# Layer 3 of a four-layer kernel: VectorE's state sums read B·dtx from PSUM, and C's spread gets one pair of banks instead of two

## The chip, the cores and the metric

The kernel runs on one core of a Trainium2 chip. Five engines work side by side, each through its own list of instructions in order: TensorE (PE, matrix products into PSUM), VectorE (DVE), ScalarE (ACT), GpSimd (POOL) and SyncE (SP), which here issues the transfers. PSUM has eight banks of 128 x 512 float32. The metric is the device time of one execution in microseconds (us), the median of several.

## The reference

Four layers follow each other on an image x of 2 x 128 channels x 64 x 64: a scan over the image in four directions, two attention layers, and a small scan over channels. The change lies in the last. There, the 128 channels of each pixel are read as 8 tokens of 16 numbers, and a selective scan runs over the 8 tokens:

```python
dA  = exp(dt[..., None] * A)
dBx = dt[..., None] * Bm[:, :, None, :] * xs[..., None]
def step(h, inp):
    dA_t, dBx_t, C_t = inp
    h = dA_t * h + dBx_t
    return h, einsum('nds,ns->nd', h, C_t)
y = ys + xs * D;  y = y * silu(z);  out = y @ out_proj_w.T
```

Each pixel has 32 inner channels with 16 states each, 512 state values per pixel and token. Behind the scan stand a group norm, a SiLU and the sum with x.

## The kernel before

Layer 3 takes the pixels in 16 chunks of 512 (8 for each image). A chunk's 8 tokens are worked in 4 steps, k = 0 to 3, of two tokens each, o = 0 and 1. A token's 512 state values times 512 pixels stand as a tile of 128 partitions x 4 groups x 512; most instructions take half of that, 128 x 1024, called half 0 or 1.

The tiles:

- D[k, o], in SBUF, is loaded from DRAM with B spread over the partitions (L1395). A product with rx turns it into B·dtx (`db_`, L1417), and a sum with A turns it into the state h (`add`, L1439). There are six buffers of it.
- rx, in PSUM, holds dt·xs of one token, spread by TensorE (`rx_`, L1413). It has two banks.
- A[k, o] is exp(dt·A) by ScalarE (`da_`, L1424). GpSimd multiplies it by the state of the token before (`mul`, L1434): A·h. This is then what the sum takes, and what is multiplied by C.
- q, in PSUM, holds C of two groups, spread by TensorE (`pc_`, L1451) for one product by C. It has two buffers of a pair of banks each.
- The product by C (`hc_`, L1457) is made in place in A, on VectorE. TensorE then sums it over the states into y (`y_`, L1467), a bank of its own. The part of y that comes from B·dtx is added apart, as (sum of C·B)·dtx (`cbx_`, `ecb_`, L1403), so that the last token's B·dtx is never needed.
- misc, one bank, takes every other matmul of the layer.

So q has four banks, rx two, y and misc one each: all eight.

The order is written out by hand. For each step s the loop goes through four groups g, and `PLAN[k][g]` names the state work in order: `m10` is GpSimd's product for token o = 1, half 0; `v10` the sum on VectorE and `g11` the sum on GpSimd, for token and half; `C` the next product by C, which belongs to the step before (`pc_` = step s-1); `D` the next product with rx, which belongs to the step after (`nc_` = step s+1). A group with a C in it first issues one more fill of q (`prepare`), ahead of the y matmuls and of what `first` lists; what `extra` lists comes behind. Each engine gets its instructions in the order in which the loop comes past them, and waits by semaphores for the others.

In a chunk there are 14 GpSimd products, 12 sums (8 on VectorE, 4 on GpSimd), 14 products with rx and 14 by C. In step k = 0 only token 1 has a predecessor within the chunk, and a product by C takes two groups of that token, whose two matmuls into q read the same 32 partitions; otherwise the two matmuls read different ones.

Transfers go by SP's queue: per step, the spread of dt (`spread`, L1383) and the loads of D for the step after the next (`load`, L1395).

## Time and profile before

| what | before |
|---|---|
| median of 3 runs | 6422.57 us (6415.79 to 6423.95) |
| the profiled execution | 6431.21 us, its span 6429.4 us |
| granted TensorE clock, whole span | 0.904 |
| busy, whole span: PE, DVE, ACT, POOL | 89%, 88%, 69%, 84% |
| layer 3, 5465.1 to 6429.4 | 964.3 us |
| busy in layer 3: PE, DVE, ACT, POOL | 834.1, 878.2, 460.9, 791.8 us |
| granted clock in layer 3 | 0.86 |

A row of a view by windows gives a stretch (us from the span's start), its length, the busy time of PE, of its weight loads, of DVE, ACT and POOL with the number of instructions, then the granted clock, the busy share of the 16 transfer engines and GB/s. A row of the groups gives line, engine, operation, tiles (written <- read), shapes and count, then the busy time in us and the mean in ns, then the idle time of the engine ahead of these instructions and what ended it. A row of the timeline gives start, duration, engine, line, tiles and shapes, and in brackets the idle time before it with what ended that. PE shows a float32 matmul of 512 columns as two records.

### The profile page before, as it was taken

The numbers are of one execution on the slowest core, as the hardware profiler recorded it, in microseconds if no ns is written. First come the engines' busy times: TensorE is split into PE (matmuls) and PEld (weight loads), VectorE is DVE, ScalarE is ACT, GpSimd is POOL, SyncE is SP. The second block draws the span as 40 slices with busy tenths as digits, with TensorE's granted clock in tenths as the row PEclk, the third lists the DMA queues.
The fourth block names the chain that finished last, engine by engine and source line by source line (L and its number), as shares of the span: only waits on it lengthen the run. The fifth ranks groups of instructions, "written<-read, shape, count | busy, mean of one in ns | idle before, by whom it ended". The sixth has DMA issues, their size and how long they took to land. (4 is left out here: it accounts for less than half of the span.)

```text
span 6429.4 us, 66778 instructions
## 1 busy us (share of the span) xinstructions
PE 5699.0 (89%) x20010; PEld 2783.6 (43%) x20010; DVE 5639.6 (88%) x4502; ACT 4413.5 (69%) x7768; POOL 5391.6 (84%) x2519
## 2 busy tenths in 40 slices
PE   8888888888888888888878999999999999888898
PEld 2222222222222222222225888888888788222221
DVE  7999999999999999999997777777777777899997
ACT  7887778877788877787776566555556665545453
POOL 6999999999999999999996677666766566888886
PEclk8888888888888988888878999999999999799887
DMA  6566666566666666666651000000000000977775
GB/s 182 144 154 168 166 152 149 147 151 151 145 149 150 156 151 152 148 155 157 153 144 42 1 5 3 1 1 1 1 1 1 2 6 7 219 184 176 182 176 123
DMA packets 400478, 700.37 MB, mean 109 GB/s; under 512 B 74089, under 2 KB 76658, under 8 KB 399730
## 3 DMA queue, kind: packets, MB, share of 16 engines
q1 hardware_dynamic: 399232, 694.33, 44.5%
q8 instruction: 157, 2.57, 0.2%
q14 instruction: 207, 1.70, 0.1%
q10 hardware_dynamic: 882, 1.78, 0.1%
HBM read 584.53 MB, written 111.28 MB: 108 GB/s over the span
## 5 line engine op out<-in xcount | busy, mean ns | idle before, releaser
L405 POOL TENSOR_TENSOR dbu<-dus,bs 128x1024 f32<-128x1024 f32 x1024 | 2463.4, 2441 | 116.6 <-DVE h L449 97.2
L449 DVE TENSOR_TENSOR_SCAN h<-da,hst,dbu 128x1024 f32<-128x1024 f32 x896 | 2088.9, 2343 | 109.5 <-ACT hst L454 46.6
L418 ACT ACTIVATE da<-dts,aneg 128x512 f32<-128x512 f32 (+1 forms) x2048 | 1411.5, 689 | 210.3 <-DVE h L449 171.2
L1028 POOL TENSOR_TENSOR sum<-sum,sc 128x1024 f32<-128x1024 f32 x378 | 898.1, 2376 | 397.9 <-ACT sc L1023 392.7
L990 ACT COPY sc<-s 128x512 f32<-128x512 f32 x1024 | 596.9, 585 | 703.2 <-PE s L985 574.9
L985 PE MATMUL s<-q,k 128*128 128x256 f32 x4096 | 1051.9, 380 | 10.3 <-ACT lo L943 5.5
L1040 PE MATMUL av<-sc,v 128*128 128x256 f32 x4096 | 1050.3, 379 | 9.1 <-ACT sc L1023 9.1
L472 PE MATMUL y<-hc,cst 128*32 128x512 f32 x4096 | 744.9, 663 | 274.3 <-DVE hc L461 245.3
L997 DVE TENSOR_TENSOR mx<-mx,s 128x512 f32<-128x512 f32 x896 | 609.8, 681 | 369.8 <-ACT sc L990 362.3
L461 DVE TENSOR_TENSOR hc<-h,pc 128x1024 f32<-128x1024 f32 x728 | 870.9, 1196 | 0.6 <-PE pc L438 0.5
L985 PEld LDWEIGHTS s<-q,k 128*128 128x128 f32 x4096 | 770.9, 190 | 124.5 <-issue 8.3
L1040 PEld LDWEIGHTS av<-sc,v 128*128 128x128 f32 x4096 | 772.1, 190 | 116.2 <-ACT sc L1023 14.4
L459 POOL TENSOR_TENSOR hc<-h,cs 128x1024 f32<-128x1024 f32 x296 | 705.1, 2382 | 1.1 <-issue 1.1
L1434 POOL TENSOR_TENSOR A<-A,D 128x1024 f32<-128x1024 f32 x224 | 526.7, 2370 | 134.3 <-DVE D L1439 100.5
L438 PE MATMUL pc<-xd,sel 16*128 16x512 f32 x1024 | 627.3, 699 | 1.3 <-DVE hc L461 1.3
L1020 DVE TENSOR_TENSOR sc<-sc,pm 128x1024 f32<-128x1024 f32 x512 | 620.7, 1213 | 2.2 <-PE pm L1015 1.7
L1023 ACT ACTIVATE sc<-sc 128x1024 f32<-128x1024 f32 x512 | 543.3, 1061 | 43.6 <-DVE sc L1020 43.4
L472 PEld LDWEIGHTS y<-hc,cst 128*32 128x32 f32 x4096 | 109.5, 112 | 805.6 <-DVE hc L461 418.4
L433 ACT ACTIVATE dbu<-hst,dbu,df 128x1 f32<-128x1 f32 x896 | 338.5, 378 | 100.3 <-POOL dbu L405 77.5
L1451 PE MATMUL q<-xs,room 32*128 32x512 f32 x840 | 287.5, 696 | 64.7 <-DVE A L1457 63.5
L438 PEld LDWEIGHTS pc<-xd,sel 16*128 16x128 f32 x1024 | 164.7, 198 | 377.4 <-issue 332.4
L449 DVE TENSOR_TENSOR_SCAN h<-da,dbu 128x1024 f32<-128x1024 f32 x128 | 290.8, 2281 | 16.0 <-POOL dbu L405 5.9
(317 smaller groups left out, 7841.9 us busy)
## 6 DMA issues: line engine op xcount, KB each, us to landing
dts<-ddt SPq DMA_DIRECT2D x512, 256.0 KB, 5.5
dus<-ddu SPq DMA_DIRECT2D x512, 256.0 KB, 5.1
D<-rows SPq DMA_DIRECT2D x448, 256.0 KB, 6.0
bs<-rows SPq DMA_DIRECT2D x1024, 64.0 KB, 4.9
cs<-rows SPq DMA_DIRECT2D x1024, 64.0 KB, 3.3
ddt<-dt SPq DMA_DIRECT2D x128, 256.0 KB, 2.0
ddu<-dtu SPq DMA_DIRECT2D x128, 256.0 KB, 4.1
dtr<-ddt SPq DMA_DIRECT2D x448, 64.0 KB, 2.1
```

What stands on the lines that cost most here:

```text
L405: nc.gpsimd.tensor_mul(t, self.dus[q], _bc(self.bs[g], 1, [P, 2, T]))
L418: act(t[:, i, sl], self.dts[q][:, i, sl], AF.Exp, scale=an[:, g, 2 * q + i : 2 * q + i + 1])
L438: mm(t, lhsT=sel[32:48, 4 * g : 4 * g + 4, :].rearrange("p n d -> p (n d)"), rhs=self.xd[32:48, :], start=True, stop=True)
L449: nc.vector.tensor_tensor_scan(ho, ai, bi, init, ALU.mult, ALU.add)
L459: nc.gpsimd.tensor_mul(t, self.h[u], _bc(self.cs[gq(u)[0]], 1, [P, 2, T]))
L461: nc.vector.tensor_mul(t, self.h[u], _bc(self.pc[u // 2], 1, [P, 2, T]))
L472: mm(self.y[q // 2][r : r + 32, :], lhsT=sum4, rhs=self.hc[u][:, i, :], start=False, stop=(u % 8 >= 6), skip_group_check=True)
L985: mm(p[:, o, :], lhsT=j.k[m // 8][:, m % 8 * P : m % 8 * P + P], rhs=self.q, start=True, stop=True)
L997: nc.vector.tensor_max(self.mx, self.s[0][:, 0:2, :] if u == 1 else self.mx, self.p[u])
L1020: nc.vector.tensor_sub(s, s, _bc(self.pm[:, :], 1, [P, 4, NQ]))
L1028: self.adds.tensor_add(self.sum, self.s[0] if w == 1 else self.sum, self.s[w])
L1040: mm(self.av, lhsT=self.job.v[m // 8][:, m % 8, :], rhs=self.s[u // 2][:, m % 4, :], start=(m == 0), stop=(m == 31))
```

## The change

VectorE's sum no longer finds B·dtx in D. The product with rx is made directly ahead of it, in the token's own step, and writes a new PSUM tile dd of two banks; the sum reads dd and A and writes D. For tokens and halves whose sum is GpSimd's, and for a chunk's first token, the product still works in place in D: it is named `d` when it belongs to the own step, `n` when it is the first token of the next chunk. The banks for dd come from q, which has one pair now. A fill of q is issued directly behind the product by C that empties the pair, instead of ahead of the group. rx is filled one token at a time, token 1 at the own step's group 0, token 0 at group 2 of the step before. `PLAN` has 9 sums on VectorE and 3 on GpSimd, in a new order.

```diff
-            def db_(self, k, o, half):
-                d = self.D[k, o][:, 2 * half : 2 * half + 2, :]
-                nc.vector.tensor_mul(d, d, _bc(self.rx[k, o], 1, [P, 2, T]))
+            def db_(self, k, o, half, own=False):
+                d = t = self.D[k, o][:, 2 * half : 2 * half + 2, :]
+                if own:
+                    t = self.dd = ps.tile([P, 2, T], F32, tag="dd", name="dd")
+                nc.vector.tensor_mul(t, d, _bc(self.rx[k, o], 1, [P, 2, T]))
...
-                eng.tensor_add(d, d, self.A[k, o][:, g, :])
+                eng.tensor_add(d, self.dd if eng is nc.vector else d, self.A[k, o][:, g, :])
...
-                q = self.q[k, u] = ps.tile([P, 2, T], F32, tag="q", name="q", bufs=2)
+                q = self.q[k, u] = ps.tile([P, 2, T], F32, tag="q", name="q")
...
         PLAN = (
-            ("m10 m11 C D", "C D time", "C v10 D", "g11 D C"),
-            ("m00 m01 C D v00", "C v01 D m10 m11", "v10 D", "g11 D"),
-            ("m00 m01 C D v00", "C v01 m10 m11", "C v10 D", "g11 C"),
-            ("m00 m01 C D", "C v00 D g01 m10 m11", "C D", "D C"),
+            ("m10 m11 C", "v10 C time", "v11 C", "C"),
+            ("m00 m01 C v00", "v01 m10 m11 C", "v10", "d11 g11"),
+            ("m00 m01 C v00", "C v01 m10 m11", "C v10", "C d11 g11"),
+            ("m00 m01 C v00", "d01 g01 m10 m11 C", "n0 C", "n1 C"),
         )
...
+                if k == 3 and nc_ is not None:
+                    more((3, 0), lambda: nc_.rx_(0, 0), at=first)
+                elif k < 3:
+                    if cc is not None:
+                        more((k, 0), lambda: cc.rx_(k, 1), at=first)
+                    if nc_ is not None:
+                        more((k, 2), lambda: nc_.rx_(nk, 0), at=first)
...
-                    more((k, 3), lambda: n2.rx_(n2k, 0), lambda: n2.rx_(n2k, 1))
...
-                    if "C" in ops:
-                        prepare()
...
                             c_.hc_(k_, u_)
                             used += 1
-                        elif o == "D":
-                            nc_.db_(nk, nd // 2, nd % 2)
-                            nd += 1
+                            prepare()
+                        elif o[0] == "n":
+                            nc_.db_(0, 0, int(o[1]))
+                        elif o[0] == "d":
+                            cc.db_(ck, int(o[1]), int(o[2]))
...
                         else:
+                            if o[0] == "v":
+                                cc.db_(ck, int(o[1]), int(o[2]), own=True)
                             cc.add(ck, int(o[1]), int(o[2]), V if o[0] == "v" else G)
```

More of the change, by code (lines that the diff above doesn't have):

```diff
@@ L1575, in conv_seq_kernel @@
                 c.load(0, o)
-            for o in range(2):
-                c.rx_(0, o)
             c1.xs = xs1
@@ L1639, in conv_seq_kernel @@
                         more(at_, lambda j=j: nrm.store(j, (G, V)[j % 2]))
-                nd = 0
                 for g in range(4):
@@ L1646, in conv_seq_kernel @@
                     if nc_ is None:
-                        ops = [o for o in ops if o != "D"]
+                        ops = [o for o in ops if o[0] != "n"]
                     if cc is None:
-                        ops = [o for o in ops if o[0] not in "mvg"]
-                    if "C" in ops:
-                        prepare()
+                        ops = [o for o in ops if o[0] not in "mvgd"]
                     if pc_ is not None and pk and g:
```

## The prediction

> **What bounds the kernel now.** I read first the busy shares and the strip of 40 slices: layer 3 is the last 964 us (5465 to 6429), VectorE (DVE) is its fullest engine, and the granted clock (PEclk) is uneven there.

> ```profile
> DVE  7999999999999999999997777777777777899997
> POOL 6999999999999999999996677666766566888886
> PEclk8888888888888988888878999999999999799887
> ```

> Then one chunk by windows, from one VectorE product L1403 to the same product of the next chunk; behind it, two stretches with the clock in them.

> ```profile
> 5803.86:5859.61 55.75, 50.60 (x160) 12.61 (x158) 54.07 (x42) 28.66 (x34) 49.48 (x21) 0.91 0.85 190
> 5808.40:5811.80 3.40, 1.65 (x6) 0.30 (x4) 3.40 (x5) 2.75 (x4) 3.29 (x2) 1.00 0.71 164
> 5811.80:5815.20 3.40, 3.40 (x8) 0.69 (x6) 3.40 (x4) 1.80 (x2) 3.40 (x2) 0.50 1.02 230
> 5839.10:5842.50 3.40, 1.29 (x4) 0.46 (x6) 3.40 (x4) 2.28 (x3) 3.40 (x2) 1.00 1.08 213
> 5842.50:5849.40 6.90, 6.90 (x14) 1.43 (x12) 6.85 (x4) 3.86 (x4) 5.52 (x3) 0.51 0.60 131
> ```

> A chunk takes 55.75 us, of which VectorE works 54.07, TensorE 50.60, GpSimd (POOL) 49.48: VectorE sets the pace and the two others are close. A 3.4 us stretch in which TensorE is busy half or less (1.65, 1.29) is followed by one or two at a clock of 0.5.

> Third, the groups of lines in layer 3, shapes kept apart.

> ```profile
> L1434 POOL TENSOR_TENSOR A<-A,D 128x1024 f32<-128x1024 f32 x224 | 526.7, 2370 | 134.3 <-DVE D L1439 100.5 <-DMA dtr<-ddt 28.7 <-DMA D<-rows 3.8
> L1439 DVE TENSOR_TENSOR D<-D,A 128x1024 f32<-128x1024 f32 x128 | 297.9, 2327 | 5.2 <-POOL A L1434 4.6
> L1457 DVE TENSOR_TENSOR A<-A,q 128x1024 f32<-128x1024 f32 x224 | 268.6, 1209 | 14.5 <-PE q L1451 14.5
> L1417 DVE TENSOR_TENSOR D<-D,rx 128x1024 f32<-128x1024 f32 x224 | 268.4, 1210 | 31.6 <-PE q L1451 15.7 <-DMA D<-rows 13.9 <-PE rx L1413 2.0
> L1439 POOL TENSOR_TENSOR D<-D,A 128x1024 f32<-128x1024 f32 x64 | 184.3, 2879 | 3.7
> ```

> The sum on VectorE (L1439, both operands in SBUF) takes 2327 ns; the products of the same size with one operand in PSUM take 1210. Last, single rows of the timeline.

> ```profile
> 5804.99 2.36 POOL L1439 TENSOR_TENSOR D<-D,A 128x1024 f32<-128x1024 f32 x1
> 5805.60 2.83 DVE L1439 TENSOR_TENSOR D<-D,A 128x1024 f32<-128x1024 f32 x1
> ...
> 5803.08 0.67 DVE L1472 TENSOR_TENSOR sz<-sz,y 128x512 f32<-128x512 f32 x1
> 5803.86 0.70 DVE L1403 TENSOR_TENSOR y<-e,misc 128x512 f32<-128x512 f32 x1
> ...
> 5816.64 1.22 DVE L1417 TENSOR_TENSOR D<-D,rx 128x1024 f32<-128x1024 f32 x1 [1.42 <-PE q L1451]
> ...
> 5823.63 1.98 PE L1451 MATMUL q<-xs,room 32*128 32x512 f32 x4
> ...
> 5842.26 1.85 PE L1451 MATMUL q<-xs,room 32*128 32x512 f32 x4 [2.11 <-DVE A L1457]
> ...
> 5849.52 1.13 PE L1451 MATMUL q<-xs,room 32*128 32x512 f32 x4
> 5850.57 1.06 PE L1467 MATMUL y<-A,cst 128*32 128x512 f32 x6
> 5851.56 1.13 PE L1451 MATMUL q<-xs,room 32*128 32x512 f32 x4
> ```

> GpSimd's sum ends at 5807.35 and VectorE's, begun in the meantime, at 5808.43, 1.08 later: it stood until GpSimd was through. L1403 overwrites what L1472 read, and starts 0.11 after its end, where products without such a tie start 0.08 before the end of the last: a tie on VectorE costs 0.19. A TensorE item (a pair for q, the rows of one y) takes a slot of 1.03 at full clock ((5851.56-5849.52)/2), twice that at half; a q pair for a chunk's first token, whose two matmuls share rows, 1.91.

> **The change, part by part.** (a) VectorE's sums read dd in PSUM. Eight a chunk go from 2.33 to 1.13 (1.21 less the overlap of 0.08): -9.6. A ninth comes from GpSimd: +1.13 here, -2.88 there; the other three there fall from 2.88 to about 2.35. Each of the nine sums waits for its own product, a tie: 9 x 0.19 = +1.7. VectorE's work in a chunk: 14 products by C and 14 by dtx at 1.13, 9 sums at 1.13, 1.7 of ties, and 4.2 of smaller ones (yg, ecb twice, cb, bn): 47.5. GpSimd's 19 operations come to 19 x 2.36 = 45. The price of a write to PSUM in this shape is not in the trace; nearest is L1403, which writes y there at 696 ns against 678 of L1472, so between 0 and 0.04 a product; I take 0.

> [...]

> (b) One pair of banks for q. The refill can start only when the product by C (I number them C1 to C14 from step k=1 on) is through. From the rows: refill starts 0.06 after the end of C, the next C 0.03 after the recorded 1.13 of the refill: C_next = refill start + 1.16 (2.01 for a first token). But the refill also stands behind what TensorE is given between two refills. VectorE's cover is what it has to do between two Cs: 2.45 for a product and its sum, 1.13 for a product in place. I walk one chunk, clock full, taking the later of (previous C + 1.13 + cover) and the refill, whose start is the later of (previous C + 1.27) and (previous refill + its slot + 1.03 per item between):
> - C2, C3: cover 6.3 and 3.6, no wait (C2 at 7.43, C3 at 12.14).
> - C4: six items ahead of its refill (xs, y0, two sz, two rx), and 0.8 in which one of them waits for ScalarE to empty misc (the timeline has 0.78 for it at 5835.00): refill at 8.70 + 7 x 1.03 + 0.8 = 16.71, ready 17.87. GpSimd is later: the product d11 ends at 12.2, only then GpSimd's g11 and m00 (2 x 2.35) run, so add v00 starts at 16.95 where VectorE was ready at 14.55. Wait 2.40, C4 at 18.12.
> - C5: y and two xr ahead: 0.29. C6, C7: none (C7 at 28.43).
> - C8: the same chain d11, g11, m00, less 0.65 for bn: 1.75.
> - C9, C10: cover 1.13 (n0, n1), one and two items: 0.17 and 0.83. C11: cover none, y and y0 ahead: 1.96.
> - C12: y, rx, bc ahead of a cover of 2.45: 0.54. C13: none. C14: cover 0.6: 0.70.
> - next C1: no cover, a first token's refill: 2.15.

> Waits for TensorE 6.64, for GpSimd 4.15, with 47.5 of work: 58.3 a chunk, +2.55. TensorE's slots (31 items and 14 refills, 48) and GpSimd's 45 both fit into it; it is the hand-over between the three that is long. Behind a waiting C stand VectorE's product and sum, for which GpSimd's next product waits; behind a waiting refill stand y and the small matmuls that ScalarE reads, which is half idle (28.66 of 55.75) and covers that.

> (c) rx goes out one at a time, seven a chunk, where three pairs and a single shared rows' time before; it is in the item counts above. Moving products a step later gives the D loads 10 us more (13.9 us of waits in the layer, under 1 a chunk, at most that is won; I take 0, the loads being issued where they were). SP's queue and ScalarE's get nothing new.

> (d) The clock. The walk leaves TensorE idle 2.8 us before the refill after C2, and 4.5 before the one after C8. By the windows above (half idle in 3.4 us) the second falls to 0.5 for certain, the first in some 8 of 10 positions of the stretch. One stretch of 3.4 us at half loses 1.7: after C8 that lands on C10 and C11, which have no cover (+1.7); after C2 on the six items before C4, of which GpSimd's wait hides 0.25 (0.8 x 1.45 = 1.2). I take +2.9 a chunk; bounds 0 and, with two stretches each as after 5842.5, 6.6. The 55.75 of before holds its own such stretches.

> [...]

> Sum: 58.3 + 2.9 - 55.75 = +5.45 a chunk, times 15 (of 16, the last has no successor to prepare) = +82. The profiled execution took 6431.2 (span 6429.4): 6513. It stands 8.6 above the median 6422.6, so 6504 there.

> **The rivals.**
> - Faster. VectorE's freed time is kept: the three chains through GpSimd and TensorE overlap better than my walk. It decides where waits fall below 55.75 - 47.5 = 8.25 a chunk. With no wait for GpSimd and four rx beside other matmuls (as 5815.48 shows rx beside q), the walk gives 54.2 without half clock: -1.55 x 15 = -23, 6400. For it: the lock on the sums is plain. Against: C11 and C1 have no cover, 4.1 by themselves, and half clock stretches occur already before.
> - No change: full clock throughout and no wait for GpSimd gives 55.8, within 0.2% (the least that a measurement here tells from nothing; 6410 to 6435).
> - Slower still: TensorE at half clock for two stretches each time: 58.3 + 6.6 - 55.75 = 9.15 x 15 = +137, 6560. For it: 5842.5 to 5849.4. Against: 5811.8 lasted one.
> - The sums do not get shorter: were dd read as slowly as D (2.33), 9 x 1.12 more work, 10.1, less the waits that it covers (at most 10.8): between +82 and +233, 6504 to 6655. Against: L1457 and L1417 at 1.21 beside a busy GpSimd.

> **How the numbers follow.** Forecast and its neighbours (6435 to 6540) 0.65; half clock worse, 0.14; sums not shorter, 0.02; no change 0.06; faster 0.13. That gives slower 0.81, same 0.06, faster 0.13. Range 6432 to 6565: it leaves out the faster case and most of no change, and takes in the bounds of the clock.

> **What would show it.** Right: VectorE's sums at about 1.21 and GpSimd's at 2.36; products by C idle behind q for 100 us or more in the layer, against 14.5; VectorE's sums waiting 40 to 80 for GpSimd, against 5; chunks at 60 to 62; VectorE's share of layer 3 lower, a granted clock at or under 0.86 there. Wrong: chunks under 55, or q refilled before VectorE asks for it at C11 and C1; then the walk's coupling is not there.

## The result

The changed kernel takes 6567.57 us (median of 4 runs, 6559.99 to 6570.9), the kernel before 6421.15 (4 runs, 6415.79 to 6423.95): a ratio of 1.0232 [1.0217, 1.0247], slower by 146 us. The forecast was 6504 within 6432 to 6565, so the sign was right, the size too small by 64 us, and the time lies 2.6 us above the range.

In the profiled execution of the changed kernel (6559.99 us, span 6558.2) layer 3 takes 1104.0 us (5454.2 to 6558.2) where it took 964.3. The first three layers, which the change does not touch, took 5454.2 there against 5465.1; those 11 us are a difference between executions.

### The profile page after: what moved, and what is told of

Read it like the earlier page. It is cut to its first block, busy times and chain, and to the rows that moved or that the text cites. A ratio compares the mean times of both kernels' runs of the same rounds, so it can differ in the third digit from the quotient of the medians.

```text
span 6558.2 us, 66859 instructions
## 1 busy us (share of the span) xinstructions
PE 5836.9 (89%) x20010; PEld 2821.6 (43%) x20010; DVE 5533.3 (84%) x4518; ACT 4412.8 (67%) x7768; POOL 5288.2 (81%) x2503
## 5 line engine op out<-in xcount | busy, mean ns | idle before, releaser
L449 DVE TENSOR_TENSOR_SCAN h<-da,hst,dbu 128x1024 f32<-128x1024 f32 x896 | 2087.2, 2341 | 98.3 <-ACT dbu L433 47.5
L1459 DVE TENSOR_TENSOR A<-A,q 128x1024 f32<-128x1024 f32 x224 | 272.4, 1216 | 201.5 <-PE q L1453 201.4
L1453 PE MATMUL q<-xs,room 32*128 32x512 f32 x840 | 318.0, 761 | 57.7 <-DVE A L1459 57.7
```

The costliest lines, as they stand in the source:

```text
L449: nc.vector.tensor_tensor_scan(ho, ai, bi, init, ALU.mult, ALU.add)
```

## The profile after

The strip of 40 slices: layer 3 is the last six to seven digits, now lower on VectorE (DVE) and GpSimd (POOL), and with a granted clock (PEclk) at 6 to 8 tenths.

```profile
DVE  7999999999999999999997777777677777776776
POOL 6999999999999999999986776666766666666664
PEclk8888888888888888888879999999999998887786
```

VectorE no longer sets the pace. In the groups of layer 3, shapes kept apart (count | busy us, mean ns of one | idle us ahead of them and who ended it):

```profile
L1459 DVE TENSOR_TENSOR A<-A,q 128x1024 f32<-128x1024 f32 x224 | 272.4, 1216 | 201.5 <-PE q L1453 201.4
L1441 DVE TENSOR_TENSOR D<-dd,A 128x1024 f32<-128x1024 f32 x144 | 176.4, 1225 | 83.5 <-POOL A L1436 71.5 <-DVE dd L1419 0.5
L1419 DVE TENSOR_TENSOR dd<-D,rx 128x1024 f32<-128x1024 f32 x144 | 176.1, 1223 | 19.9 <-PE rx L1413 14.1 <-DMA D<-rows 4.4 <-DMA dtr<-ddt 1.5
L1441 POOL TENSOR_TENSOR D<-D,A 128x1024 f32<-128x1024 f32 x48 | 113.3, 2361 | 127.1 <-PE q L1453 55.3 <-DVE D L1419 29.4 <-issue 26.2
```

VectorE's sums fell from 2327 to 1225 ns and GpSimd's from 2879 to 2361. In the kernel before an instruction of GpSimd ended during 104 of VectorE's 128 sums, and each of the 104 ended 1.08 to 1.09 us behind that end; the other 24 took 1.21 to 1.22 us. Of GpSimd's 64 sums the 37 that began while one of VectorE's ran took 3.2 to 3.4 us, the others 2.3 to 2.4, one 2.8. This is what the prediction calls the lock, and in the changed kernel it is gone: 63 of VectorE's 144 sums began while GpSimd was at work, and all 144 took 1.22 to 1.23 us. One of the 24, with both operands in SBUF, but between two instructions of GpSimd:

```profile
5831.72 2.35 POOL L1434 TENSOR_TENSOR A<-A,D 128x1024 f32<-128x1024 f32 x1 [1.17 <-DVE D L1439]
5834.08 1.22 DVE L1439 TENSOR_TENSOR D<-D,A 128x1024 f32<-128x1024 f32 x1
5835.38 2.35 POOL L1434 TENSOR_TENSOR A<-A,D 128x1024 f32<-128x1024 f32 x1 [1.30 <-DMA dtr<-ddt]
```

In place of the lock VectorE stands 201.4 us behind q (14.5 before) and 71.5 us behind GpSimd's products (4.6 before).

One chunk by windows (span, then busy us of PE, PEld, DVE, ACT, POOL with instruction counts, then granted clock, DMA share, GB/s), and in it three stretches ahead of and behind C9:

```profile
5855.47:5921.45 65.98, 58.71 (x158) 14.87 (x158) 47.22 (x44) 28.54 (x33) 44.37 (x20) 0.84 0.67 151
5893.50:5896.90 3.40, 0.72 (x4) 0.00 (x0) 1.93 (x3) 0.18 (x1) 3.40 (x2) 1.00 1.06 214
5896.90:5903.70 6.80, 5.83 (x13) 0.96 (x13) 5.76 (x6) 0.00 (x0) 5.20 (x4) 0.50 0.81 175
5903.70:5910.50 6.80, 6.80 (x13) 1.65 (x12) 1.79 (x2) 4.55 (x5) 6.73 (x4) 0.50 1.00 221
```

VectorE's work is 47.22, GpSimd's 44.37 (the walk: 47.5 and 45); the chunk is 65.98 all the same. After a stretch in which TensorE was busy 0.72 of 3.40 the clock goes to 0.50 and stays there for 13.6 us, although TensorE is busy in 12.63 of those. That is what the waits on VectorE's row show (start, length, instruction, wait ahead of it):

```profile
5860.07 1.22 DVE L1459 TENSOR_TENSOR A<-A,q 128x1024 f32<-128x1024 f32 x1 [2.07 <-PE q L1453]
5861.21 1.22 DVE L1419 TENSOR_TENSOR dd<-D,rx 128x1024 f32<-128x1024 f32 x1
5862.54 1.23 DVE L1441 TENSOR_TENSOR D<-dd,A 128x1024 f32<-128x1024 f32 x1
...
5877.16 1.22 DVE L1441 TENSOR_TENSOR D<-dd,A 128x1024 f32<-128x1024 f32 x1 [2.56 <-POOL A L1436]
5880.11 1.22 DVE L1459 TENSOR_TENSOR A<-A,q 128x1024 f32<-128x1024 f32 x1 [1.72 <-PE q L1453]
5894.86 1.23 DVE L1441 TENSOR_TENSOR D<-dd,A 128x1024 f32<-128x1024 f32 x1 [1.98 <-POOL A L1436]
5901.91 1.22 DVE L1459 TENSOR_TENSOR A<-A,q 128x1024 f32<-128x1024 f32 x1 [1.04 <-PE q L1453]
5907.78 1.22 DVE L1459 TENSOR_TENSOR A<-A,q 128x1024 f32<-128x1024 f32 x1 [3.51 <-PE q L1453]
5912.30 1.22 DVE L1459 TENSOR_TENSOR A<-A,q 128x1024 f32<-128x1024 f32 x1 [3.30 <-PE q L1453]
```

The rows are C1, a product with its sum, v00, C4, v00 of the last step, C9, C10 and C11. TensorE's rows show the two gaps, ahead of the refill for C3 (its first row) and ahead of y behind C8's refill (its second), and what TensorE is busy with behind the second: `32*128` and `128*32` are the rows and columns of the array that a matmul uses.

```profile
5868.80 1.36 PE L1453 MATMUL q<-xs,room 32*128 32x512 f32 x4 [2.46 <-DVE A L1459]
...
5897.63 1.92 PE L1469 MATMUL y<-A,cst 128*32 128x512 f32 x4 [3.41 <-DVE y L1403]
5899.79 2.08 PE L1453 MATMUL q<-xs,room 32*128 32x512 f32 x4 [0.24 <-DVE A L1459]
5901.80 1.92 PE L1469 MATMUL y<-A,cst 128*32 128x512 f32 x4
5903.65 2.08 PE L1314 MATMUL misc<-xs,room 128*128 128x512 f32 x2
5905.65 2.08 PE L1453 MATMUL q<-xs,room 32*128 32x512 f32 x4
5907.66 1.92 PE L1469 MATMUL y<-A,cst 128*32 128x512 f32 x4
5909.52 1.61 PE L1462 MATMUL y<-xs,room 128*128 128x512 f32 x2
5911.06 1.13 PE L1453 MATMUL q<-xs,room 32*128 32x512 f32 x4
```

At half clock a refill of q takes 2.08 and each item ahead of it 1.9 to 2.1; the last row is back at 1.13. Over layer 3 the time at half clock, read from the clock records stretch by stretch, went from 275 to 445 us and the mean granted clock from 0.86 to 0.80.

## The experiments

Medians, ratios to the kernel before on the same chip with their 95% intervals (the ratios are what compares across chips), and of the profiled execution the length of layer 3, its time at half clock and the waits of VectorE's products by C for q (us; a dash where it is not used below):

| kernel | median | ratio | layer 3 | half clock | waits for q |
|---|---|---|---|---|---|
| before | 6421.2 | 1 | 964 | 275 | 14.5 |
| after | 6567.6 | 1.0232 [1.0217, 1.0247] | 1104 | 445 | 201 |
| old order, one pair | 6526.5 | 1.0180 [1.0165, 1.0196] | 1068 | 399 | 126 |
| new order, two pairs, in place | 6674.1 | 1.0412 [1.0395, 1.0429] | 1225 | 717 | 85 |
| new order, one pair, in place | 6665.3 | 1.0412 [1.0374, 1.0450] | 1245 | 716 | - |
| gaps filled, 32-row tiles | 6573.4 | 1.0253 [1.0235, 1.0271] | 1114 | 424 | - |
| gaps filled, full tiles | 6500.8 | 1.0128 [1.0112, 1.0144] | 1046 | 213 | - |
| d11 ahead of v10 | 6510.0 | 1.0157 [1.0139, 1.0175] | 1057 | 361 | 218 |
| the same, TensorE's items moved | 6510.2 | 1.0141 [1.0124, 1.0158] | 1032 | 336 | 175 |
| + rx from 64 rows | 6439.0 | 1.0029 [1.0017, 1.0041] | 970 | 154 | 119 |
| + rx from 128 rows | 6414.7 | 1.0013 [1.0004, 1.0023] | 958 | 150 | 114 |
| + product and sum apart | 6422.9 | 1.0022 [1.0012, 1.0031] | 973 | 196 | 128 |
| before, rx from 64 rows | 6503.2 | 1.0130 [1.0115, 1.0145] | 1041 | 348 | - |

The last three columns belong to single executions. The one of the new order with one pair, in place, took 6712.8 us, 48 above its median; the one of the moved items 6498.0, 12 below.

### The parts of the change, one by one

The old order with one pair of banks for q, refilled directly behind the product that empties it:

```diff
-                q = self.q[k, u] = ps.tile([P, 2, T], F32, tag="q", name="q", bufs=2)
+                q = self.q[k, u] = ps.tile([P, 2, T], F32, tag="q", name="q")
...
-                    if "C" in ops:
-                        prepare()
...
                             c_.hc_(k_, u_)
                             used += 1
+                            prepare()
```

> The kernel before with one pair of banks for q, its refill issued directly behind the product by C; order, products and sums as before, so two banks of PSUM lie idle. Theory A (a pair costs where VectorE has nothing to do between two products by C): the old order has a product or a sum between almost any two of them (cover 1.13 to 4), so waits of 0.2 to 1 at some ten places, and half clock on top: 3 to 8 us a chunk, 6465 to 6540. Rival B (it is the new order that costs, not the pair): 6420 to 6440.

6526.5 us, 1.0180 [1.0165, 1.0196]: the pair alone costs 118 us against the 6408.9 of the kernel before on the same chip. It fits theory A. VectorE waits 125.6 us for q (14.5 before). Its sums, still in SBUF, are somewhat shorter (2145 ns against 2327). If those that meet an instruction of GpSimd cost what they did before (2583 ns in the mean, the others 1218), some 87 of the 128 meet one instead of 104, an estimate:

```profile
L1439 DVE TENSOR_TENSOR D<-D,A 128x1024 f32<-128x1024 f32 x128 | 274.6, 2145 | 0.2
```

The new order with two pairs and the product in place in D, without dd:

```diff
                 d = t = self.D[k, o][:, 2 * half : 2 * half + 2, :]
-                if own:
-                    t = self.dd = ps.tile([P, 2, T], F32, tag="dd", name="dd")
...
-                eng.tensor_add(d, self.dd if eng is nc.vector else d, self.A[k, o][:, g, :])
+                eng.tensor_add(d, d, self.A[k, o][:, g, :])
...
-                q = self.q[k, u] = ps.tile([P, 2, T], F32, tag="q", name="q")
+                q = self.q[k, u] = ps.tile([P, 2, T], F32, tag="q", name="q", bufs=2)
```

The first refill is made twice ahead of the loop, so that two pairs are always ahead.

> The changed kernel's order with two pairs of banks for q and the product with rx in place in D (no dd). Theory A (the pair is the loss): the 201 us that VectorE waits for q go, and nine sums a chunk take 2.3 again instead of 1.2, 10 us a chunk or 150 in all: about 6520. Rival B (the order loses by itself: a product directly ahead of its sum keeps VectorE behind GpSimd, and a locked sum holds GpSimd's next product): 6570 or more.

6674.1 us, 1.0412 [1.0395, 1.0429], far slower than either kernel. The new order loses by itself, and a second pair does not save it; the rival holds and my number for the other theory missed; the sums in place took 1810 ns, not the 2.3 us that it counted with. VectorE's sums wait for GpSimd as long as in the changed kernel:

```profile
L1439 DVE TENSOR_TENSOR D<-D,A 128x1024 f32<-128x1024 f32 x144 | 260.6, 1810 | 84.1 <-POOL A L1434 71.8 <-DVE D L1417 0.5 <-POOL e L1371 0.5
```

and 84.7 us go to waits for q even with two pairs, 70.5 to rx, 49 to y: TensorE is at half clock for 717 of 1225 us.

The new order with one pair, and still without dd:

```diff
# from the changed kernel
                 d = t = self.D[k, o][:, 2 * half : 2 * half + 2, :]
-                if own:
-                    t = self.dd = ps.tile([P, 2, T], F32, tag="dd", name="dd")
...
-                eng.tensor_add(d, self.dd if eng is nc.vector else d, self.A[k, o][:, g, :])
+                eng.tensor_add(d, d, self.A[k, o][:, g, :])
```

> The changed kernel with the product with rx in place in D instead of dd; one pair of banks for q and the order stay. It gives the price of dd alone. Theory A (VectorE sets the pace between its waits): nine sums at 2.3 instead of 1.2, 10 us a chunk, 6700 to 6720. Rival B (the longer sums fill time in which VectorE waits for q anyway): 6570 to 6620.

6665.3 us, 1.0412 [1.0374, 1.0450], between the two expectations. So in the new order reading the sums from PSUM is worth 98 us by the medians and 115 by the ratios, which were taken on different chips, and a second pair without dd nothing that can be told (6674.1 against 6665.3). The parts do not add up: the order with products in place costs 265 us (6674.1 - 6408.9), dd gives some 100 back, and the pair costs 118 in the old order and none on top of the new. What goes with these losses in the table is the time at half clock (717 and 716 us in the two runs in place), and that is what the next runs ask about.

### What holds the clock down

The prediction has the clock fall after a gap and return after one busy stretch. If gaps in time were all, TensorE given more to do in its two gaps would keep full speed. First with repeats of the small matmul that spreads rx, which write the same values into the same bank:

```diff
+            def again_(self, k, o, n):
+                i, j = PLACE[k]
+                r = slice(32 * (j + o), 32 * (j + o) + 32)
+                for _ in range(n):
+                    mm(self.rx[k, o], lhsT=rep[r, :], rhs=self.e[r, i, :], start=True, stop=True)
...
+                if cc is not None and k == 1:
+                    more((1, 1), lambda: cc.again_(1, 1, 2), at=first)
+                if nc_ is not None and k == 3:
+                    more((3, 0), lambda: nc_.again_(0, 0, 3))
```

> The changed kernel with five extra matmuls a chunk that write rx once more with the values it already holds: two in the gap of TensorE ahead of the refill for C3, three in the one ahead of the refill for C9. Nothing is computed differently. Theory A (the part of the loss that the forecast sized too small is the half clock that these two gaps bring on, 6.6 us a chunk instead of 2.9): the time at half clock in layer 3 falls from 445 us to under 200, chunks go from 64.9 to about 59, the time to about 6480. Rival B (the hand-over of the one pair of banks costs the same at any clock, the low clock is a symptom): five more slots of TensorE gain nothing, 6560 or more.

6573.4 us, 1.0253 [1.0235, 1.0271]: nothing won. That is rival B's number, but the test that it needs, the same time without half clock, was not made by this run: half clock stayed (424 us, 445 in the changed kernel). Of fourteen chunks six took 61.0 to 61.3, three 65.8 to 67.4, three 72.8, and the two around the change of image 73.5 and 75.2. Windows of one at 72.8, behind them one at 61.2 (columns as above):

```profile
5764.30:5767.70 3.40, 3.13 (x11) 1.05 (x10) 1.41 (x3) 0.86 (x2) 3.40 (x2) 1.00 1.06 214
5767.80:5784.80 17.00, 15.45 (x28) 3.11 (x28) 8.02 (x8) 4.55 (x5) 15.23 (x8) 0.50 0.94 199
5784.80:5801.90 17.10, 17.10 (x38) 3.17 (x36) 9.09 (x8) 10.97 (x11) 6.56 (x3) 0.50 0.23 78
5867.18:5928.40 61.22, 56.81 (x168) 14.81 (x168) 47.06 (x45) 28.56 (x33) 44.41 (x20) 0.94 0.69 163
```

The clock falls behind a stretch in which TensorE was busy 3.13 of 3.40 us (a gap of 1.69 us begins at its end), and it stays at 0.5 for 34.1 us, of which the second half is busy without a break. Busy time alone does not bring full speed back, and my theory of the clock fell.

A new one (theory C): what counts is how much of the 128 x 128 array is in use. A refill of q or a spread of rx uses 32 of 128 rows, a sum for y 32 of 128 columns. I cut the clock records into stretches of 3.41 us and took for each of the 4029 that lie in layer 3, in the traces of all thirteen kernels, the sum of duration x rows x columns / 16384 over its matmuls, as a share of the stretch (overlapping records can bring it above 1, as to 1.24 in the stretch from 5872.98 of the changed kernel):

| stretch | count | busy, median | array share, quartiles |
|---|---|---|---|
| half clock, full clock given back behind it | 336 | 1.00 | 0.83 / 0.99 / 1.18 |
| half clock, stays at half | 1037 | 1.00 | 0.44 / 0.58 / 0.78 |
| full clock, falls behind it | 349 | 0.50 | 0.20 / 0.34 / 0.46 |
| full clock, stays full | 2307 | 1.00 | 0.60 / 0.76 / 0.86 |

Busy time does not tell the upper two rows apart; the share of the array does, at its ends. Of the stretches at half clock that were busy throughout (0.99 or more), full speed came back behind 3 of 317 with a share under 0.6, behind 170 of 563 between 0.6 and 1.0, and behind all 156 above. In between the share of one stretch does not settle it: in the chunk shown the clock stayed at half behind a stretch with 0.90 and came back behind the next, with 0.70. And this is a correlation. The test is to fill the same gaps with full tiles. Here one and three matmuls of the whole array write into rx's bank ahead of one true spread; they are overwritten, and nothing of the computation is left out:

```diff
+            def full_(self, k, o, n):
+                for _ in range(n):
+                    mm(self.rx[k, o], lhsT=ident, rhs=self.xs[:, 0, :], start=True, stop=True)
+                i, j = PLACE[k]
+                r = slice(32 * (j + o), 32 * (j + o) + 32)
+                mm(self.rx[k, o], lhsT=rep[r, :], rhs=self.e[r, i, :], start=True, stop=True)
...
+                if cc is not None and k == 1:
+                    more((1, 1), lambda: cc.full_(1, 1, 1), at=first)
+                if nc_ is not None and k == 3:
+                    more((3, 0), lambda: nc_.full_(0, 0, 3))
```

> The changed kernel with matmuls of the whole array (128 rows by 128 columns) in the two gaps of TensorE that the run with 32-row fillers used, one and three, each followed by the spread of rx once more, so that rx holds what it held: six slots against five there. Theory C (what lets the clock fall and keeps it down is the share of the array in use, not the time in use; small tiles, 32 rows for q and rx, 32 columns for y, count little): time at half clock well under the 424 us of the 32-row fillers, under 300, hardly a chunk over 70 us, 6490 to 6530. Rival D (only time in use counts, fillers cost their slots): as the 32-row fillers or worse, 6570 or more.

6500.8 us, 1.0128 [1.0112, 1.0144]: 73 us less than with small tiles in the same two gaps (80 by the ratios; six slots a chunk against five), and half clock at 213 us where it was 424. That is what theory C expects, but the two runs differ in more than the tiles. The full tiles close the second gap; the small ones, of which one shares q's slot (0.69 us beside q's 0.70), leave 1.69 us of it (TensorE waits ahead of y for VectorE's L1403: 25.3 us in layer 3 with small tiles, 2.8 with full ones, 50.0 in the changed kernel). So this pair does not part the share of the array from the time in use; the widths of rx, below, do. A chunk at full clock throughout, by windows, and three of VectorE's rows in it:

```profile
5719.50:5778.30 58.80, 55.99 (x170) 14.94 (x170) 47.10 (x45) 28.62 (x34) 43.72 (x20) 1.00 0.75 170
```

```profile
5724.15 1.22 DVE L1466 TENSOR_TENSOR A<-A,q 128x1024 f32<-128x1024 f32 x1 [2.07 <-PE q L1460]
5741.24 1.22 DVE L1448 TENSOR_TENSOR D<-dd,A 128x1024 f32<-128x1024 f32 x1 [2.56 <-POOL A L1443]
5769.11 1.22 DVE L1466 TENSOR_TENSOR A<-A,q 128x1024 f32<-128x1024 f32 x1 [1.94 <-PE q L1460]
```

These are C1, v00 and C11: 2.07, 2.56 and 1.94 where the walk has 2.15, 2.40 and 1.96, and the chunk is 58.8 where the walk has 58.3. In the kernel before, an ordinary chunk took 56.3 in the mean, with its own half clock in it (twelve from one L1351 of VectorE to the next, without the two around the change of image). Against that the change costs 2.5 a chunk at full clock, some 38 us over 15; the other 102 of the 140 us in layer 3 I put down to the low clock, by this difference alone.

### The wait for GpSimd

The other named wait is VectorE's add v00 behind GpSimd's g11 and m00, which wait for VectorE's product d11. Here d11 is put ahead of v10:

```diff
-            ("m00 m01 C v00", "v01 m10 m11 C", "v10", "d11 g11"),
-            ("m00 m01 C v00", "C v01 m10 m11", "C v10", "C d11 g11"),
+            ("m00 m01 C v00", "v01 m10 m11 C", "d11 g11 v10", ""),
+            ("m00 m01 C v00", "C v01 m10 m11", "C d11 g11", "C v10"),
```

> The changed kernel with one thing moved: VectorE's in-place product d11 stands ahead of v10 (step k=1) or of v10 and its product by C (k=2), so that GpSimd's sum g11 can start behind m11. Theory A (the chain d11, g11, m00 costs the walk's 4.15 us a chunk): VectorE's waits for GpSimd in its sums fall from 71 us to under 15, and half or more of that is won, 6500 to 6540. Rival B (the refill of q is due at the same places and takes the wait over): the waits for GpSimd fall as well, those for q grow by as much, 6550 to 6575.

6510.0 us, 1.0157 [1.0139, 1.0175], as the theory of that chain expects: 58 us won by the medians, 48 by the ratios. The wait of the sums for GpSimd (71.5 us) is 0.7; the products by C wait more instead. The view of waits of the changed kernel, then of this one (total us, count, longest):

```profile
DVE A L1459 <- PE q L1453: 201.4, 115, 5.8
DVE D L1441 <- POOL A L1436: 71.5, 32, 2.6
```

```profile
DVE A L1459 <- PE q L1453: 218.0, 115, 8.2
```

Next, the same order with TensorE's items put where its gaps are: xs for the second half moved one place up, the future chunk's dt with its exp and ln from (3, 2) to (3, 0), y0 from (3, 3) to (3, 1):

```diff
+                if fut2 is not None:
+                    more((3, 0), lambda: fut2.dt_(1), fut2.e_exp, fut2.e_ln, at=first)
...
-                    more((3, 3), lambda: cc.y0_(1), at=first)
+                    more((3, 1), lambda: cc.y0_(1), at=first)
...
-                    more((1, 2), lambda: fut2.xs_(1), at=first)
+                    more((1, 1), lambda: fut2.xs_(1), at=first)
...
-                if fut2 is not None:
-                    more((3, 2), lambda: fut2.dt_(1), fut2.e_exp, fut2.e_ln, at=first)
```

> The changed kernel with work moved, none added: the in-place product d11 goes ahead of v10, so that GpSimd's sum g11 need not wait for it; the second xs matmul goes into TensorE's gap ahead of the refill for C3; dt's second matmul goes ahead of cbx in step k=3 and y0's second ahead of the refill for C9, away from the refills for C10 and C11, which have no cover. Theory A (the loss sits at the places that the walk names): some 4 us a chunk less at full clock and less half clock, 6440 to 6490. Rival B (the single pair loses by its hand-over wherever it stands): 6540 or more.

6510.2 us, 1.0141 [1.0124, 1.0158], between the two expectations. Against the run above layer 3 is 25 us shorter in the profiled executions, while the medians do not differ (6510.0 and 6510.2); nor do the intervals of the ratios; nothing can be claimed for the moves by themselves. Half clock is 336 us.

### More of the array for the same work

Theory C says that the same spread of rx, read from more rows with zero weights in the extra ones, costs no time and keeps the clock up. To the version just shown:

```diff
-                mm(q, lhsT=rep[r, :], rhs=self.e[r, i, :], start=True, stop=True)
+                r = slice(64 * ((j + o) // 2), 64 * ((j + o) // 2) + 64)
+                mm(q, lhsT=(ident, odd)[(j + o) % 2][r, :], rhs=self.e[r, i, :], start=True, stop=True)
```

The two weights are made once, ahead of the loop: 32 rows hold rep, the other 32 zeros.

> The run with the moved work, and rx spread from 64 rows instead of 32, by weights that are zero in the other 32: the same result and the same slot of 1.03 us, twice the share of the array. Theory C: less half clock than that run, 15 to 40 us faster than it. Rival D (only time in use counts): the same time as that run, or slower by slots that rx shared with q, up to 30 us.

6439.0 us, 1.0029 [1.0017, 1.0041]: 71 us less than with 32 rows, where I had expected 15 to 40. Half clock fell from 336 to 154 us (the expectation below has 158). And here TensorE's gaps stayed: between the first and the last L1351 of VectorE in layer 3, gaps of 1 us or more were 17 in each run, 26.6 us together with 32 rows and 31.0 with 64, while the falls of the clock went from 19 to 5. So it is not the time in use that the wider tile changed, but the share of the array.

With all 128 rows, three quarters of the weights zero:

```diff
-                r = slice(64 * ((j + o) // 2), 64 * ((j + o) // 2) + 64)
-                mm(q, lhsT=(ident, odd)[(j + o) % 2][r, :], rhs=self.e[r, i, :], start=True, stop=True)
+                mm(q, lhsT=wide[j + o], rhs=self.e[:, i, :], start=True, stop=True)
```

The four weights `wide` are made ahead of the loop, and some small tiles are moved into free columns of another to make room.

> The run with the moved work (d11 early, xs, dt and y0 in TensorE's gaps) and rx spread from all 128 rows, by weights that are zero in 96 of them, instead of 64 or 32; same result, same slots. Theory C (the share of the array in use decides on the clock): half clock under 120 us in layer 3, against 158 with 64 rows and 336 with 32; chunks at 53 to 55; 6405 to 6430. Rival D (only time in use counts): 6440 or more, since rx can no longer run beside q.

6414.7 us, 1.0013 [1.0004, 1.0023], as expected in the time; half clock was to fall under 120 and is 150, and the ordinary chunks took 54.1 to 58.0 where 53 to 55 were expected. Twice the share brought hardly less half clock than 64 rows did (150 against 154; 11 falls behind 18 gaps of 1 us or more, 30.9 us together). This is the fastest version with the change in it; by the ratios it gains some 10 us on 64 rows (24 by the medians, on different chips), and it does not beat the kernel before. Layer 3 as a whole, the changed kernel and this one, each with VectorE's products by C:

```profile
5454.20:6558.20 1104.00, 975.50 (x2520) 247.11 (x2518) 774.22 (x718) 460.19 (x513) 711.58 (x306) 0.80 0.66 154
```

```profile
5454.60:6412.60 958.00, 845.89 (x2520) 226.33 (x2518) 776.32 (x733) 460.56 (x514) 713.32 (x306) 0.92 0.75 178
```

```profile
L1459 DVE TENSOR_TENSOR A<-A,q 128x1024 f32<-128x1024 f32 x224 | 272.6, 1217 | 118.3 <-PE q L1453 113.8
```

VectorE's and GpSimd's work are the same to about 2 us; the granted clock went from 0.80 to 0.92, and with it and with the moved work 146 us went. Still 113.8 us go to waits for q.

To give some of the places without cover one, product and sum of the first token were pulled apart by a product by C:

```diff
-            ("m10 m11 C", "v10 C time", "v11 C", "C"),
+            ("m10 m11 C p10", "C a10 time", "C p11", "C a11"),
```

> As the run with rx from 128 rows, and in step k=0 the product and the sum of v10 and v11 are pulled apart with a product by C between them, so that three of the uncovered refills get 1.1 to 1.7 us of cover. Theory A (uncovered refills are the rest of the loss): 5 to 25 us faster than that run. Rival B (TensorE has more to do in that step than VectorE, so that its refills come late with any cover): the same time, within 5 us.

6422.9 us, 1.0022 [1.0012, 1.0031], 8 us more than the run before by the medians, with intervals that overlap. The 5 to 25 us of theory A were not won; whether the time is the same within 5 us, as the rival has it, these runs do not tell. Waits for q rose to 128.3 and half clock to 196 us. In step k=0 TensorE is the late one (in one chunk it works without a gap from 5862.0 to 5874.4, through four refills of q), so dividing VectorE's cover differently does not refill q sooner; why half clock rose stays open.

Last, the rows of rx alone, on the kernel before:

```diff
# on the kernel before
-                mm(q, lhsT=rep[r, :], rhs=self.e[r, i, :], start=True, stop=True)
+                r = slice(64 * ((j + o) // 2), 64 * ((j + o) // 2) + 64)
+                mm(q, lhsT=(ident, odd)[(j + o) % 2][r, :], rhs=self.e[r, i, :], start=True, stop=True)
```

> The kernel before with rx spread from 64 rows. Theory C: time at half clock in layer 3 from 275 us to under 200, and of the 46 us that VectorE waits for q and rx a part gone: 6390 to 6412. Rival D: 6415 to 6450, rx no longer shares its slot with its pair.

6503.2 us, 1.0130 [1.0115, 1.0145], slower by 86 us, and both expectations missed. In the kernel before, two spreads of different 32 rows ran at the same time in one slot; reading the same 64 rows, they go one after the other. The pair before, then the two in this run, at full clock both:

```profile
5826.52 1.19 PE L1413 MATMUL rx<-e,cst 32*128 32x512 f32 x4
```

```profile
5802.35 1.12 PE L1414 MATMUL rx<-e,cst 64*128 64x512 f32 x2
5803.32 1.02 PE L1414 MATMUL rx<-e,odd 64*128 64x512 f32 x2
```

VectorE waits for the slots that this takes: its products by dtx 32.1 us for rx (2.0 before), its product with y (L1473, L1472 before) 61.8 us for y (8.1 before). Half clock rose to 348 us. In layer 3 of the changed kernel 199 of the 224 records of rx have no other matmul beside them for more than 0.3 us, in the kernel before 34. The wider tile won 71 us on the changed kernel with its items moved, and lost 86 on the kernel before.

## Why the prediction was right or wrong

- **VectorE's work and the sums: right.** 1225 and 2361 ns against the 1.21 and 2.36 us foretold, 47.2 us of work a chunk against 47.5. A product into PSUM took 1223 ns, 13 more than the 1210 in place before and within the 0 to 40 allowed. (The terms given for VectorE's work add up to 47.7, not 47.5.) The tie between a product and its sum is there: sums without another wait follow their product 0.11 after its end (the product of 5861.21, 1.22 long, and its sum at 5862.54).
- **Where the sum reads B·dtx from:** the sum at 5834.08 of the kernel before, from SBUF alone, took 1.22 us, and the sums with dd, from PSUM, took 1225 ns.
- **The walk at full clock: right.** 58.3 a chunk against 58.8 where the clock stayed at 1.00, with the single waits named there within 0.2 us. In the changed kernel's own chunk C1 waits 2.07 (2.15), v00 2.56 (2.40) and 1.98 (1.75). The chain d11, g11, m00 cost 48 to 58 us by the run without it; the prediction has 4.15 a chunk, 62 us. The waits for GpSimd were foretold as 40 to 80 us and came to 71.5.
- **(d) The clock: the step that failed.** Taken at +2.9 a chunk, with one stretch of 3.4 us at half after each gap. In the chunk shown C4 waits 1.72 more than the walk, C9 0.87, C10 2.68 and C11 1.34: 6.6 together. The gaps of TensorE were where the walk put them (2.46 us ahead of the refill for C3 and 3.41 behind C8's, against 2.8 and 4.5), and the clock fell at both; what was wrong is the return. I let one busy stretch bring full speed back, as behind 5811.80; behind 5842.50 it had taken two. The clock records of the kernel before had said so: of 26 falls between the first and the last L1351 of layer 3, 9 lasted one stretch, 12 two, and 5 three or four. In the changed kernel 1 of 28 lasted one, 13 two, 13 three or four, and one 18: hardly more falls, but longer ones. Behind these gaps TensorE is busy, but in part with tiles of 32 rows or columns, and in the chunk shown full speed came back after two and after four stretches (6.8 and 13.65 us).
- **What that comes to.** Chunks were to take 60 to 62. Counted from one L1351 to the next, the twelve ordinary ones took 64.5 in the mean, 6.2 over the walk, and 56.3 before, 0.55 over the one chunk that the sum took as its base: +8.2 a chunk where the sum has +5.45, which makes 34 of the 58 us by which layer 3 grew more than forecast. The two chunks around the change of image, 73.9 and 80.9 against 62.0 and 68.1 before, give 14 more, and the two ends of the layer the rest; the sum took both for ordinary chunks.
- **Short gaps** came ahead of half clock too: 2.46 us ahead of C3's refill in the changed kernel, 1.69 in the run with 32-row fillers. And busy time alone did not bring full speed back: 17.10 of 17.10 us busy at 0.50.
- **The rivals.** "Slower still" is what happened: its condition (two stretches each time) is the one that the trace shows at C4, with four at C9, and its price of 6.6 a chunk is what the four waits above add up to; 6560 against 6567.6. It had 0.14. That the time comes so near is in part luck: its +9.15 a chunk is more than the 8.2 of ordinary chunks, and the chunks around the change of image make up for it. The "faster" rival failed on the two waits that spoke against it, C11 and C1, and on the clock. The range ended 5 us above the worst clock allowed, with no room for an error of the walk beside it, which was 0.5 a chunk.
- **What the forecast did not say: how the parts stand to each other.** It priced the pair at 6.64 and GpSimd's wait at 4.15 a chunk as if either could be taken away alone. By the runs the pair costs 118 us in the old order, and in the new order without dd a second pair gives nothing back: TensorE is at half clock there for 717 us with two pairs and for 716 with one.

What stays open: theory C rests on the three widths of rx (336, 154 and 150 us of half clock) with TensorE's gaps the same, and on the share in the clock stretches; the fillers (424 to 213) fit it, but closed a gap besides. How the share is taken by the chip, and over what time, these runs do not show: between 0.6 and 1.0 one stretch does not tell whether full speed returns. And no run widened q, whose two matmuls share a slot from different rows (1.13 us for both at 5911.06 in the changed kernel), so that what its 32 rows cost was not tried.

## What to carry to other kernels

Where VectorE sets the pace and TensorE hands it banks, count for each product the cover that is left between its bank's emptying and its next use; with one pair of banks, the places without cover waited 2.07 us (C1) and 1.94 (C11) even at full clock, and the time freed on VectorE did not pay that back. Look at TensorE's clock records before a change opens gaps: here gaps of 2.5 and 3.4 us were followed by 6.8 and 13.7 us at half speed, with small tiles among what came next. And look at all of the falls in the record, not at two. Where a small matmul stands alone in its slot, try it on more rows with zero weights, which took 82 us (by the ratios) to 95 (by the medians) off here for no more matmuls; where it shares the slot with another, leave it: in the kernel before, the same cost 86 us.
